# One transfer queue taking loads and stores in turns, and a looped TensorE program, in a per-sample matmul with residual

## The chip, the cores and the metric

The kernel runs on one core of a Trainium2 chip. The metric is the device time of one execution in microseconds. Three executions of the kernel before gave a median of 328.17 us (328.01 to 328.28). A further execution was recorded by the hardware profiler; it took 328.11 us. The profile's span, from the first to the last instruction that it shows, is 326.2 us, so 1.9 us of that execution lie outside the span.

## The reference

`x` is 128 samples of 128 channels by 1024 time steps, float32 (67.1 MB). Each sample has a subject number from 0 to 7, and each subject has a 128x128 float32 weight matrix. The sample is multiplied by the transposed matrix of its subject, and the product is added to the sample:

```python
w = weights[subjects]                       # (128, 128, 128): one matrix per sample
out = jnp.einsum('bct,bcd->bdt', x, w)      # per sample: w^T (d x c) times x (c x t)
return x + out
```

Every sample has to be read from HBM once and written back once: 134.2 MB together, to which the weights add 0.5 MB.

## The kernel before

A tile of the work is two samples (`G = 2`), 1 MB, and there are `NT = 64` tiles. One sample of a tile is 512 KB: 128 partitions of 1024 floats. Tiles live in 23 slots of SBUF (`SLOTS`, line 32); the result is written in place over the loaded samples, and the slot is then stored. PSUM holds four products of 128x1024 floats (`P_SLOTS`), and four buffers hold the weight matrix of a sample (`W_SLOTS`).

Each engine has its own instruction stream, written out by hand, and the streams meet only at semaphores:

- **SyncE (SP)** first loads all eight weight matrices (line 127), then issues two 512 KB loads per tile (lines 128 to 140). For the first 23 tiles it keeps a lead of three: before it issues tile i it waits until tile i-3 has landed (line 133). From tile 23 on it waits until the store that last used the slot has landed (line 131).
- **GpSimd (POOL)** reads the sample's subject number into a register (line 148), and copies that subject's matrix into one of the four weight buffers (line 158). From the fifth sample on it first waits until the product that used the buffer four samples ago is done (line 157).
- **TensorE (PE)** waits for the tile's load (line 145), the weight copy (line 160) and, from the fifth sample on, for the PSUM buffer to be free (line 162). It then does two matmuls of 128x512 (line 164). A float32 matmul shows as two MATMUL records in the profile, so one tile is eight of them. Its program is written out in full: 256 matmuls in a row. Three matmuls on zeros run ahead of it (line 111).
- **VectorE (DVE)** adds the product in PSUM to the sample in its slot, 128x1024 (line 174).
- **ScalarE (ACT)** issues one 1 MB store per tile when both its samples have been added (lines 177 to 183).

Thus loads sit in SP's DMA queue and stores in ACT's. Both queues are served by the same 16 DMA engines. In the profile, all loads and stores of samples carry line 53, which is the helper `transfer`; SP's are loads, ACT's are stores. At the end SP waits for the last 23 stores (line 187).

For one of the 16 DMA engines, a tile's load is four packets of 16 KB, and a tile's store is eight packets of 8 KB.

Of the kernel before, what the change touches and what calls it, by code (L numbers as in the profile page):

```python
# [1 line left out]

# [4 lines left out]

F32 = mybir.dt.float32
I32 = mybir.dt.int32
ALU = mybir.AluOpType


G = 2

N = 512  # L30

SLOTS = 23

W_SLOTS = 4
P_SLOTS = 4
DMA = 16

LEAD = 3

IDLE = 3  # L40

ROWS = 4
QUEUES = {mybir.EngineType.SP: "qSPDynamicHW", mybir.EngineType.Activation: "qActDynamicHW"}


def transfer(nc, engine, out, in_):

    later, nc._always_lower_symbolic_ap = nc._always_lower_symbolic_ap, False  # L50
    ins, outs = engine.lower_ap_dma(in_), engine.lower_ap_dma(out)
    nc._always_lower_symbolic_ap = later
    return engine.add_instruction(  # L53
        mybir.InstDMACopy(
            name=nc.get_next_instruction_name(),
            engine=engine.engine,
            ins=ins,
            outs=outs,
            mode="Copy",
            cce_op=ALU.bypass,  # L60
            queue=QUEUES[engine.engine],
        )
    )


@with_exitstack
def kernel(
    ctx: ExitStack,
    tc: tile.TileContext,
    x: bass.AP,  # L70
    subjects: bass.AP,
    weights: bass.AP,
    out: bass.AP,
):
    nc = tc.nc
    B, C, T = x.shape
    S, _, D = weights.shape
    NT = B // G

    def sbuf(name, *shape, dtype=F32):  # L80
        return ctx.enter_context(nc.sbuf_tensor(name, list(shape), dtype)).ap()

    given, near, wrap, index = (
        sbuf(name, 1, B, dtype=I32) for name in ("given", "near", "wrap", "index")
    )
    w_all = sbuf("w_all", C, S, D)
    ws = [sbuf(f"w{i}", C, 1, D) for i in range(W_SLOTS)]
    zeros = sbuf("zeros", C, N)
    xs = [sbuf(f"x{i}", C, G, T) for i in range(SLOTS)]
    ps = [  # L90
        ctx.enter_context(nc.psum_tensor(f"ps{i}", [D, T], F32)).ap() for i in range(P_SLOTS)
    ]

    s_given = tc.alloc_semaphore("s_given")
    s_wall = tc.alloc_semaphore("s_wall")
    s_index = tc.alloc_semaphore("s_index")
    s_zeros = tc.alloc_semaphore("s_zeros")
    s_copied = tc.alloc_semaphore("s_copied")
    s_product = tc.alloc_semaphore("s_product")
    s_added = tc.alloc_semaphore("s_added")  # L100
    s_load = [tc.alloc_semaphore(f"s_load{i}") for i in range(SLOTS)]
    s_store = [tc.alloc_semaphore(f"s_store{i}") for i in range(SLOTS)]

    with tc.tile_critical():  # L104

        nc.scalar.dma_start(given, subjects.rearrange("(o b) -> o b", o=1)).then_inc(s_given, DMA)

        nc.vector.memset(zeros, 0.0).then_inc(s_zeros, 1)  # L108
        nc.tensor.wait_ge(s_zeros, 1)
        for _ in range(IDLE):  # L110
            nc.tensor.matmul(  # L111
                ps[P_SLOTS - 1][:, :N], zeros[:, :D], zeros, start=True, stop=True
            )

        nc.vector.wait_ge(s_given, DMA)
        nc.vector.tensor_scalar(near, given, -S, S - 1, ALU.max, ALU.min).then_inc(s_index, 1)  # L118
        nc.vector.wait_ge(s_index, 1)
        nc.vector.tensor_scalar(wrap, near, 0, S, ALU.is_lt, ALU.mult).then_inc(s_index, 1)  # L120
        nc.vector.wait_ge(s_index, 2)
        nc.vector.tensor_tensor(index, near, wrap, ALU.add).then_inc(s_index, 1)  # L122
        nc.gpsimd.wait_ge(s_index, 3)

        nc.sync.dma_start(w_all, weights.rearrange("s c d -> c s d")).then_inc(s_wall, DMA)  # L127
        for i in range(NT):
            k, turn = i % SLOTS, i // SLOTS
            if turn:  # L130
                nc.sync.wait_ge(s_store[k], DMA * turn)
            elif i >= LEAD:
                nc.sync.wait_ge(s_load[k - LEAD], DMA * G)
            for g in range(G):
                transfer(
                    nc,
                    nc.sync,
                    xs[k][:, g, :],
                    x[i * G + g].rearrange("(a r) t -> a (r t)", r=ROWS),
                ).then_inc(s_load[k], DMA)  # L140

        nc.gpsimd.wait_ge(s_wall, DMA)
        for i in range(NT):
            k, turn = i % SLOTS, i // SLOTS
            nc.tensor.wait_ge(s_load[k], DMA * G * (turn + 1))
            for g in range(G):
                b = i * G + g
                s = nc.values_load(
                    index[0:1, b : b + 1],
                    engines=[mybir.EngineType.Pool],  # L150
                    min_val=0,
                    max_val=S - 1,
                    skip_runtime_bounds_check_because="the index is clamped on the chip above",
                )
                w, p = ws[b % W_SLOTS], ps[b % P_SLOTS]
                if b >= W_SLOTS:
                    nc.gpsimd.wait_ge(s_product, b - W_SLOTS + 1)
                nc.gpsimd.tensor_copy(w, w_all[:, bass.ds(s, 1), :]).then_inc(s_copied, 1)  # L158

                nc.tensor.wait_ge(s_copied, b + 1)  # L160
                if b >= P_SLOTS:
                    nc.tensor.wait_ge(s_added, b - P_SLOTS + 1)
                for t in range(0, T, N):
                    mm = nc.tensor.matmul(  # L164
                        p[:, t : t + N],
                        w[:, 0, :],
                        xs[k][:, g, t : t + N],
                        start=True,
                        stop=True,
                    )  # L170
                mm.then_inc(s_product, 1)

                nc.vector.wait_ge(s_product, b + 1)
                nc.vector.tensor_tensor(xs[k][:, g, :], p, xs[k][:, g, :], ALU.add).then_inc(  # L174
                    s_added, 1
                )
            nc.scalar.wait_ge(s_added, (i + 1) * G)
            transfer(
                nc,
                nc.scalar,  # L180
                out[i * G : (i + 1) * G].rearrange("g d t -> d g t"),
                xs[k].rearrange("d (o g) t -> d o (g t)", o=1),
            ).then_inc(s_store[k], DMA)


        for i in range(NT - SLOTS, NT):
            nc.sync.wait_ge(s_store[i % SLOTS], DMA * (i // SLOTS + 1))


# [1 line left out]
_INS = ["x", "itok_B_0_7", "L0_cond_weights"]  # L191
_OUTS = [((128, 128, 1024), "float32")]


# [20 lines left out]
```

## Time and profile before

| what | value |
|---|---|
| median of three executions | 328.17 us |
| the profiled execution | 328.11 us |
| its span | 326.2 us |
| moved by DMA | 134.86 MB, 413 GB/s over the span |
| TensorE, matmuls | 239.9 us busy, 74% |
| VectorE | 157.9 us busy, 48% |
| GpSimd | 37.8 us busy, 12% |
| DMA engines | busy in 38 of 40 slices of the span at nine tenths or more |

The page cuts the span into 40 slices of 8.15 us. The row "DMA" gives how busy the 16 DMA engines are in each, in tenths, and the row "GB/s" what they moved. The matmul row of TensorE counts pipelined instructions whose ends are modelled, so its busy share overstates how close that engine is to its limit. The queues in the page are numbered: q1 carries SP's transfers (loads and weights), q10 ACT's (stores), and q8 and q14 carry instructions that engines fetch while they run.

### The profile page before, as it was taken

How to read it: one execution, taken by the hardware profiler on the slowest of the kernel's cores; microseconds unless marked ns; L12 is line 12 of the kernel's file. 1: busy time of each engine (PE TensorE's matmuls, PEld its weight loads, DVE VectorE, ACT ScalarE, POOL GpSimd, SP SyncE). 2: the span in 40 equal slices, each digit the busy share in tenths (PEclk: the TensorE clock that was granted, in tenths of full speed). 3: DMA queues.
4: the chain of work that ended last, by engine and by line, in shares of the span. 5: the costliest groups of instructions: out<-in, count | busy, mean ns of one | idle time of the engine just before them, and what ended most of it. 6: DMA issues, size and time to landing. Idle time of an engine off the chain costs nothing.

```text
span 326.2 us, 1941 instructions
## 1 busy us (share of the span) xinstructions
PE 239.9 (74%) x518; PEld 94.5 (29%) x518; DVE 157.9 (48%) x132; POOL 37.8 (12%) x132
## 2 busy tenths in 40 slices
PE   6999989889899998998898898898776866000000
PEld 2444333333333333333333333333232322000000
DVE  1676665565565555665565565666445446000000
POOL 1111111111111111111111111111111110000000
PEclk9999999999999999999999999999999999655555
DMA  7999999999999999999999999999999999999993
GB/s 259 418 415 424 423 420 425 421 430 422 427 424 423 422 426 421 426 424 427 425 425 422 425 427 420 425 424 422 424 432 430 420 422 424 428 424 428 424 428 163
DMA packets 16411, 134.86 MB, mean 413 GB/s; under 512 B 3089, under 2 KB 4114, under 8 KB 4114
## 3 DMA queue, kind: packets, MB, share of 16 engines
q1 hardware_dynamic: 7184, 67.64, 49.5%
q10 hardware_dynamic: 9218, 67.11, 49.1%
q8 instruction: 4, 0.07, 0.1%
q14 instruction: 5, 0.04, 0.0%
HBM read 67.63 MB, written 67.11 MB: 413 GB/s over the span
## 4 chain that ended last, share of the span: by engine, by line
DMA 45%; SPq 24%; another core or an unknown queue 13%; PE 1%; issue 1%; DVE 0%
DMA x<-in_x_dram 30%; SPq L53 23%; DMA out_dram<-x 15%; PE ps L164 1%; DVE x L174 0%; SPq L127 0%; SPq L211 0%; SPq L104 0%
## 5 line engine op out<-in xcount | busy, mean ns | idle before, releaser
L164 PE MATMUL ps<-x,w 128*128 128x512 f32 x512 | 234.7, 604 | 34.2 <-DMA x<-in_x_dram 34.1
L174 DVE TENSOR_TENSOR x<-ps,x 128x1024 f32<-128x1024 f32 x128 | 156.7, 1224 | 117.4 <-PE ps L164 117.4
L164 PEld LDWEIGHTS ps<-x,w 128*128 128x128 f32 x512 | 92.6, 189 | 176.7 <-issue 95.2
L158 POOL COPY w<-w_all 128x128 f32 x128 | 37.6, 294 | 228.3 <-PE ps L164 222.3
L111 PE MATMUL ps<-zeros 128*128 128x512 f32 x6 | 5.2, 1035 | 1.7 <-DVE zeros L108 1.7
L111 PEld LDWEIGHTS ps<-zeros 128*128 128x128 f32 x6 | 1.8, 328 | 3.7 <-issue 2.1
L108 DVE MEMSET zeros<- 128x512 f32 x1 | 0.5, 485 | 1.1 <-SPq L104 1.1
L118 DVE TENSOR_SCALAR near<-given 1x128 int32<-1x128 int32 x1 | 0.2, 215 | 0.6 <-DMA given<-in_itok_B_dram 0.6
L122 DVE CUSTOM_DVE_ANT_0 index<-near,wrap 1x256 uint16<-1x256 uint16 x1 | 0.3, 278 | 0.0
L120 DVE TENSOR_SCALAR wrap<-near 1x128 int32<-1x128 int32 x1 | 0.2, 215 | 0.0
L202 POOL MEMSET const-float32-0.0<- 128x1 f32 x1 | 0.1, 98 | 0.2 <-issue 0.2
L202 POOL MEMSET const-bfloat16-1.0<- 128x1 bf16 x1 | 0.1, 102 | 0.0
L202 POOL MEMSET const-uint8-127<- 128x1 uint8 x1 | 0.1, 102 | 0.0
L202 POOL MEMSET const-float32-1.0<- 128x1 f32 x1 | 0.1, 98 | 0.0
## 6 DMA issues: line engine op xcount, KB each, us to landing
x<-in_x_dram SPq DMA_DIRECT2D x128, 512.0 KB, 12.0
out_dram<-x ACTq DMA_DIRECT2D x64, 1024.0 KB, 40.6
w_all<-in_L_cond_weights_dram SPq DMA_DIRECT2D x1, 512.0 KB, 4.3
given<-in_itok_B_dram ACTq DMA_DIRECT2D x1, 0.5 KB
```

Source lines behind the costliest of these rows:

```text
L53: return engine.add_instruction(mybir.InstDMACopy(name=nc.get_next_instruction_name(), engine=engine.engine, ins=ins, outs=outs, mode="Cop ...
L108: nc.vector.memset(zeros, 0.0).then_inc(s_zeros, 1)
L111: nc.tensor.matmul(ps[P_SLOTS - 1][:, :N], zeros[:, :D], zeros, start=True, stop=True)
L118: nc.vector.tensor_scalar(near, given, -S, S - 1, ALU.max, ALU.min).then_inc(s_index, 1)
L120: nc.vector.tensor_scalar(wrap, near, 0, S, ALU.is_lt, ALU.mult).then_inc(s_index, 1)
L122: nc.vector.tensor_tensor(index, near, wrap, ALU.add).then_inc(s_index, 1)
L158: nc.gpsimd.tensor_copy(w, w_all[:, bass.ds(s, 1), :]).then_inc(s_copied, 1)
L164: mm = nc.tensor.matmul(p[:, t : t + N], w[:, 0, :], xs[k][:, g, t : t + N], start=True, stop=True,)
L174: nc.vector.tensor_tensor(xs[k][:, g, :], p, xs[k][:, g, :], ALU.add).then_inc(s_added, 1)
L202: nc = _bacc.Bacc("TRN2", target_bir_lowering=False, num_devices=1)
```

## The change

All transfers of samples go into SP's queue. SP first issues the loads of five tiles (`LEAD = 5`). Then, for each tile i, it issues the load of tile i+5, and after it the store of tile i. There are 8 slots instead of 23, so from tile 8 on, the load of tile i+5 waits until the store of tile i-3 has landed. The waits of the first loads for earlier loads are gone. ScalarE issues only the one load of the subject numbers.

TensorE's program becomes a loop of 8 turns over a body of 8 slots, 16 samples or 32 matmuls. As the body has to be the same in each turn, its waits can't count upwards. A new helper, `take`, waits until a semaphore has reached a count and then lowers it by that count. TensorE no longer waits for the PSUM buffer itself. Instead GpSimd's copy of the weights of sample b waits until the addition of sample b-4 is done (it was: the product of sample b-4), and TensorE waits for that copy.

```diff
-SLOTS = 23
+SLOTS = 8
-LEAD = 3
+LEAD = 5
-QUEUES = {mybir.EngineType.SP: "qSPDynamicHW", mybir.EngineType.Activation: "qActDynamicHW"}
+QUEUES = {mybir.EngineType.SP: "qSPDynamicHW"}
+def take(engine, sem, count):
+    engine.sem_inc(sem, -count).wait_op(sem, count, "sem-ge")
...
-        for i in range(NT):
+        def load(i):
             k, turn = i % SLOTS, i // SLOTS
             if turn:
                 nc.sync.wait_ge(s_store[k], DMA * turn)
-            elif i >= LEAD:
-                nc.sync.wait_ge(s_load[k - LEAD], DMA * G)
             for g in range(G):
                 transfer(nc, nc.sync, xs[k][:, g, :], ...).then_inc(s_load[k], DMA)
+        def store(i):
+            k = i % SLOTS
+            nc.sync.wait_ge(s_added, (i + 1) * G)
+            transfer(nc, nc.sync, out[i * G : (i + 1) * G]..., xs[k]...).then_inc(s_store[k], DMA)
+        for i in range(LEAD):
+            load(i)
+        for i in range(NT):
+            if i + LEAD < NT:
+                load(i + LEAD)
+            store(i)
+        with nc.tensor.Fori(0, NT // SLOTS):
+            for k in range(SLOTS):
+                take(nc.tensor, s_load[k], DMA * G)
+                for g in range(G):
+                    j = k * G + g
+                    take(nc.tensor, s_copied, 1)
+                    for t in range(0, T, N):
+                        mm = nc.tensor.matmul(ps[j % P_SLOTS][:, t : t + N], ws[j % W_SLOTS][:, 0, :], xs[k][:, g, t : t + N], start=True, stop=True)
+                    mm.then_inc(s_product, 1)
...
-            nc.tensor.wait_ge(s_load[k], DMA * G * (turn + 1))
...
                 if b >= W_SLOTS:
-                    nc.gpsimd.wait_ge(s_product, b - W_SLOTS + 1)
+                    nc.gpsimd.wait_ge(s_added, b - W_SLOTS + 1)
...
-                nc.tensor.wait_ge(s_copied, b + 1)
-                if b >= P_SLOTS:
-                    nc.tensor.wait_ge(s_added, b - P_SLOTS + 1)
-                for t in range(0, T, N):
-                    mm = nc.tensor.matmul(...)
-                mm.then_inc(s_product, 1)
...
-            nc.scalar.wait_ge(s_added, (i + 1) * G)
-            transfer(nc, nc.scalar, out[...], xs[k]...).then_inc(s_store[k], DMA)
```

## The prediction

> **What bounds the kernel now.** I read the page's row of slices first, then the queues, then stretches of the start, the middle and the end, the waits and the order of time near the last load. The page:
>
> ```profile
> DMA  7999999999999999999999999999999999999993
> GB/s 259 418 415 424 423 420 425 421 430 422 427 424 423 422 426 421 426 424 427 425 425 422 425 427 420 425 424 422 424 432 430 420 422 424 428 424 428 424 428 163
> q1 hardware_dynamic: 7184, 67.64, 49.5%
> q10 hardware_dynamic: 9218, 67.11, 49.1%
> q8 instruction: 4, 0.07, 0.1%
> q14 instruction: 5, 0.04, 0.0%
> ```
>
> The DMA engines are full from the second slice to the last but one. 134.86 MB at 424 GB/s are 318.1 us of the 326.2. The rest is start and end. Stretches of the trace (stretch, its length, clock, DMA share, GB/s):
>
> ```profile
> 6.00:14.00 8.00, 1.00 0.99 406
> 40.00:140.00 100.00, 1.00 1.01 424
> 140.00:264.00 124.00, 1.00 1.01 424
> 285.00:318.00 33.00, 0.50 1.01 426
> 320.00:322.00 2.00, 0.50 0.52 217
> 322.00:324.00 2.00, 0.50 0.07 29
> 324.00:326.20 2.20, 0.50 0.00 0
> ```
>
> Three things are to be seen. Loads alone (6 to 14 us) run at 406, stores alone (285 to 318) at 426, both mixed from two queues at 424. The end is ragged: engines run dry from 320 us on, and from 322 to 324 us only 29 GB/s move, which is one engine's share (426/16 = 26.6). One straggler thus ends some 1.7 us after the other fifteen: in the trace's records of single packets its last packet ends at 324.1, the next engine's at 322.4, and nine engines end between 320.0 and 320.8. Then 2.1 us pass to the end of the span, and 1.9 us lie outside it (328.11).
>
> Near the last load, TensorE waits for data although it has the time (start, duration, and in brackets the idle time before):
>
> ```profile
> 267.12 3.70 PE L164 MATMUL ps<-x,w 128*128 128x512 f32 x8 [1.25 <-DMA x<-in_x_dram]
> 272.04 3.70 PE L164 MATMUL ps<-x,w 128*128 128x512 f32 x8 [1.22 <-DMA x<-in_x_dram]
> 275.78 1.23 DVE L174 TENSOR_TENSOR x<-ps,x 128x1024 f32<-128x1024 f32 x1 [0.49 <-PE ps L164]
> ```
>
> A tile takes TensorE 3.70 us of each 4.92. After it nothing computes; the last 48 us are stores. So only three things count: the rate of the 16 DMA engines, whether they ever lack work, and the ragged end.
>
> [...] the trace makes it depend on whether a load behind a store in the same queue runs like the mix or like loads alone. I go by the trace. [...] The q8 row shows four packets of 16 KB; their records lie at 44, 110, 177 and 226 us, near 1.05 us each. TensorE has the longest program (518 MATMUL and 518 LDWEIGHTS records[...]), so I take q8 to be its fetches; the page doesn't name the engine. [...]
>
> **The change part by part**, from 328.11.
>
> *Bytes.* The same. 0 us.
>
> *The queue's depth.* The order in the queue is load i+4, store i-1, then load i+5 once store i-3 has landed. Behind store i-3 stand load i+3, store i-2, load i+4 and store i-1: 4 MB, 9.9 us at 424. In that time the landing must be seen and the next load reach the engines. Issue to first packet took 1.7 us at the start (SP's first issue at 0.96, first packets at 2.7), the issue itself 0.6 us; for the landing of a store I allow 2 us, the length of the whole stretch between last packet and end of span. 4.3 us, and up to 3.3 us more for the spread between engines (320.8 to 324.1): 7.6 of 9.9. No gap: 0 us. SP's issues: 64 x (2 x 0.6 + 0.6) = 115 us of 316. Issues took up to 9.2 us before where a queue had no room; then the queue is full of work, and it costs nothing.
>
> *Stores wait on SP instead of ACT.* Behind the wait for the additions of tile i stand load i+6 and all that follows. Load i landed five loads and five stores' time before its store is due: 5 MB lie between, 12.4 us, and TensorE's 3.70, VectorE's 1.2 and the queueing before them need some 7. Nothing waits: 0 us. At the start: tiles 0 to 5 and the weights are 6.8 MB, at 406 GB/s until 2.7 + 16.7 = 19.4 us; the first store was issued at 12.86 before, and comes no later. At the end, behind the last load stand five stores, 12.4 us, against 7 us of compute: covered.
>
> *TensorE's loop.* Three lowered semaphores per tile and one branch per 8 tiles. No row shows either. Below 0.25 us each (PEld's waits for issue were at most 0.2 us), 0.8 us per tile beside 1.22 us idle; even without that cover the 12.4 - 7 us above take it. 0 us. [...]
>
> *Weights copied after the addition.* The copy of sample b now comes 1.2 us (VectorE) and 0.3 us (the copy) after product b-4; three products of 1.71 us lie between. 0 us.
>
> *Rate.* Unknown, bounded by packets. A 16 KB load packet took 640 ns while only loads ran, 616 in the mix; an 8 KB store packet 311 in either case. Now one engine gets four load packets, then eight store packets. Lower bound: the fastest mix seen early, 611 and 309, for all: 64 x (4 x 5 + 8 x 2) ns = 2.3 us less. Upper bound of rate alone: 640 for all; 24 of 256 load packets per engine were at 640 already, so 232 x 24 ns = 5.6 us more. Which? In the start, after a packet that was held up (839 to 1054 ns), the same engine did the next two to four load packets at 611 before it fell back to 640. [...] the lead lasts up to four load packets, just as many as a tile has. In the mix, one store packet between load packets was enough to keep them at 616. So I take eight stores to restore the lead: 616 and 311 as before, 0 us, with the two bounds kept.
>
> *Turning.* A queue turns 128 times between loads and stores. In the mix each engine turned some 500 times between the two queues with no gap. At the first store, though, half of the engines showed one packet longer by 0.22 to 0.26 us. If every turn to stores cost that: 64 x 0.23 = 14.7 us. I take 0.
>
> *The ragged end.* The four packets of q8, 4.2 us together, would, on one engine, put it just where it is: 4.2 us before 324.1 is 319.9, where the other early engines end. If they go, the next engine ends the run: 322.4, 1.7 us less. Bounds: 0 (q8 is another engine's or still fetched) and 3.3 (all end by 320.8).
>
> Sum: 328.11 - 1.7 = 326.4. The profiled execution is 0.06 under the median, so 326.5.
>
> **Rivals.**
> 1. *All as taken* (chance 0.50): 326.5; own range 324.5 to 327.4. For it: 424 and 426 in the trace, the lone straggler and q8's size.
> 2. *The straggler stays, rate as before* (0.15): 328.1. For it: q8 isn't named, and another engine may take the part. Against: 4.2 us fits its lateness.
> 3. *Loads fall back to the rate of loads alone* (0.20): +5.6 - 1.7, 332.0. For it: 640 ns in all loads without stores between. Against: the packets at 611 after a hold. It decides slower as soon as more than a third of the load packets fall back (1.7 / 5.6 = 0.3).
> 4. *Each turn to stores costs 0.23 us* (0.10): 341. For it: the first store's packet. Against: the mix. Over 0.03 us per turn it ends slower.
> 5. *The slots are too few* (0.05): if landing and reissue took 12 us and not 7.6, 2 us would be missing in every 4 tiles, 16 x 2.1 = 34 us, or some part of it: about 345. Against: the sum above.
>
> **How the numbers follow.** The time is case 1's. A tenth may lie beyond either side; cases 4 and 5 (0.15) are left out above, and a few hundredths below: 324.3 to 333.5, which takes in cases 1 to 3. What this kernel's measurement can tell from no change is about 0.2%, 0.66 us. Faster: case 1 and a little of 2, 0.51. Same: most of 2 and the edge of 1, 0.15. Slower: 3, 4, 5, with little else, 0.34.
>
> **What would show it.** Right: one data queue with 134.8 MB, slices at 424 or more from the second to the last but one, q8 gone or at one packet, no stretch of 2 us near 29 GB/s at the end, TensorE waiting for loads, no wait of SP for an addition with the DMA share under 0.95. Load packets at 616 confirm the rate; at 640, or slices near 415, it is case 3. Dips in each slice at full-speed packets are case 4; DMA share well under 1 with SP waiting for stores is case 5. I am wrong most easily where I took the lead of reads to be restored by stores, since no trace of one mixed queue exists here.

## The result and the profile after

The changed kernel takes 329.15 us (median of 7 executions, 329.07 to 329.69), the kernel before 328.28 us beside it (327.77 to 328.32). The ratio is 1.0034, with a 95% interval of 1.0024 to 1.0043: slower by 0.9 us, where 1.7 us less were forecast. The profiled execution took 329.49 us, its span is 327.7 us.

The page of the changed kernel, slices and queues:

```profile
DMA  7999999999999999999999999999999999999991
GB/s 250 416 418 430 410 433 418 418 434 421 415 432 420 421 428 425 422 431 422 422 433 422 424 430 422 424 431 421 426 432 420 424 434 418 427 433 418 425 425 79
q1 hardware_dynamic: 16400, 134.75, 98.3%
q14 instruction: 6, 0.05, 0.0%
q10 hardware_dynamic: 2, 0.00, 0.0%
```

All samples go through q1, q8 is gone, and the DMA engines are as full as before. Stretches of the changed kernel (stretch, length, clock, DMA share, GB/s):

```profile
6.00:14.00 8.00, 1.00 0.97 399
40.00:140.00 100.00, 0.98 1.01 424
140.00:264.00 124.00, 1.00 1.01 426
318.00:320.00 2.00, 0.50 1.00 422
320.00:322.00 2.00, 0.50 0.43 180
322.00:324.00 2.00, 0.50 0.06 25
324.00:326.00 2.00, 0.50 0.04 16
326.00:327.70 1.70, 0.50 0.02 5
```

The rate in the middle is 424 to 426 GB/s, against 424 for the mix of two queues. The difference is at the end: about one engine's share (25 GB/s; a sixteenth of 426 is 26.6) now moves not only from 322 to 324 us, but on to 325.4, where the last packet ends. The waits of SP's queue in the changed kernel (who waits, for whom, total, times, longest):

```profile
SPq L53 <- DMA out_dram<-x: 179.3, 56, 3.5
SPq L53 <- DVE x L200: 21.8, 9, 4.4
SPq L206 <- DMA out_dram<-x: 8.9, 4, 2.4
```

SP waits 56 times for a store to land, and nine times for an addition, while the DMA share stays at 1: these waits cost nothing that shows.

A store's semaphore is raised sixteen times, and the trace keeps the time of each (3088 times for the 193 transfers of SP in the changed kernel). They are read here as one for each of the 16 DMA engines. The last store's sixteen times say where the end comes from. "Middle" is the median of the sixteen, "last" the last of them, in us from the span's start:

| kernel | middle | last | last - middle | profiled execution |
|---|---|---|---|---|
| before | 321.19 | 324.48 | 3.29 | 328.11 |
| changed | 321.21 | 325.78 | 4.57 | 329.49 |

The middle engine ends at the same time. The straggler ends 1.3 us later, and the profiled execution is 1.4 us longer. Fifteen of the sixteen engines are done by 322.50. The lag of the last engine behind the middle one, from store to store in the changed kernel, is 0.34 us at tile 4, 1.03 at tile 16, 1.95 at tile 20, 2.84 at tile 32 and 4.47 at tile 56. From tile 20 on it grows by 0.07 us with every tile, and before that lies one step: 1.20 us at tile 18, 1.86 at tile 19, beside an instruction fetch of 8 KB on q14 at 117.4 us. The kernel before has a step of some 0.6 us too (tile 17, fetches of q14 at 125.9 and 126.5 us), and a growth of 0.07 to 0.08 us per tile between tiles 17 and 31, so neither is new. The growth stops when the last loads have landed (306 us in the middle engine): 4.60 at tile 60, 4.57 at tile 63.

### The profile page after: what moved, and what is told of

Same layout as the page of the kernel before. It is cut to its first block, busy times and chain, and to the rows that moved or that the text cites. A ratio compares the mean times of both kernels' runs of the same rounds, so it can differ in the third digit from the quotient of the medians.

```text
span 327.7 us, 2017 instructions
## 1 busy us (share of the span) xinstructions
PE 240.0 (73%) x518; PEld 95.1 (29%) x518; DVE 158.0 (48%) x132; POOL 38.1 (12%) x132
```

## The experiments

### Is it GpSimd's register loads, or TensorE's loop?

The subject numbers lie in one SBUF partition, and each of the 128 register loads reads there. The guess (theory R) was that this burdens one DMA engine alone; no run shows how partitions and DMA engines belong together. Four kernels: without the register loads (from the changed kernel and from the one before), with the register loads spread over 16 partitions, and with TensorE's program written out.

```diff
# e1_static, e2_before_static
-                s = nc.values_load(index[0:1, b : b + 1], ...)
+                s = b % S
...              (the copy then takes w_all[:, s : s + 1, :])
# e3_rotate: given ... index on 128 partitions, subjects broadcast to them
+                r = 64 * (b % 2) + 4 * (b // 2 % 8)
-                    index[0:1, b : b + 1],
+                    index[r : r + 1, b : b + 1],
# e4_unrolled
-        with nc.tensor.Fori(0, NT // SLOTS):
-            for k in range(SLOTS):
-                take(nc.tensor, s_load[k], DMA * G)
+            for i in range(NT):
+                k, turn = i % SLOTS, i // SLOTS
+                nc.tensor.wait_ge(s_load[k], DMA * G * (turn + 1))
                 for g in range(G):
-                    j = k * G + g
-                    take(nc.tensor, s_copied, 1)
+                    j = i * G + g
+                    nc.tensor.wait_ge(s_copied, j + 1)
...
```

> The changed kernel without GpSimd's register loads: the matrix of sample b is that of subject b modulo 8, known when the program is built, so the weights are not those of the sample's subject. Theory R (the 128 register loads from the subject numbers, which all lie in SBUF partition 0, slow the one DMA engine[...] by some 0.036 us each): the straggler goes, the last DMA engine ends some 1 us after the others and not 4.6, and the time falls by 3 to 4 us, to 325 to 326. Theory M (one DMA engine is slower in a mix of loads and stores whatever GpSimd does): no change, 329.0 to 329.4, 16 to 25 GB/s still moving between 322 and 326 us.

> The same edit in the kernel before (matrix of subject b modulo 8, so not that of the sample's subject). Theory R: its straggler (3.3 us after the middle engine) goes too, and it ends within 1.5 us of the others: 326 to 327. Theory M: 328.0 to 328.4 as before.

> The changed kernel with the subject numbers copied to all 128 partitions, and each register load taking another one of 16 partitions in turn[...]. Theory R: the delay of 4.6 us is shared by 16 engines, 0.3 us each: 325 to 326.5. Theory M: 329.0 to 329.4.

> The changed kernel with TensorE's program written out in full again, with rising wait counts (one queue, 8 slots, weights copied after the addition stay). If the loop of TensorE has a part in the loss: a time other than 329.15 by over 0.5 us, faster if it costs. If the loop only removed instruction fetches: the four 16 KB packets come back, each holding up one DMA engine by about 0.8 us, and the time is 329 to 331, by which engine they meet.

| kernel | median | ratio to before, 95% |
|---|---|---|
| e1_static | 329.10 | 1.0026 to 1.0054 |
| e2_before_static | 327.81 | 0.9988 to 1.0004 |
| e3_rotate | 329.72 | 1.0041 to 1.0068 |
| e4_unrolled | 329.19 | 1.0021 to 1.0048 |

The register loads are not the cause: theory R falls in all three. Without them the last engine still ends 4.40 us behind the middle one (e1_static) and 2.90 (e2_before_static). (In e3_rotate one engine is 2.2 us behind at tile 0 already; the broadcast of the subject numbers is probably why, and it is slower still.) TensorE's loop is worth nothing: written out, the time is 329.19 against 329.15. Its queues:

```profile
q1 hardware_dynamic: 16400, 134.75, 98.2%
q8 instruction: 4, 0.07, 0.1%
q14 instruction: 6, 0.05, 0.0%
q10 hardware_dynamic: 2, 0.00, 0.0%
```

q8 is back, so these four fetches are TensorE's, and they don't set the end: its last engine ends at 325.70 with them, and the changed kernel's at 325.78 without. Their records lie at 80, 145, 215 and 295 us, and the sixteen times of the stores show that each sets back another engine than the straggler, whose lag is, for example, 2.98 us at tile 24 and 2.96 at tile 25, before and after the second. That takes away the forecast's 1.7 us.

### One queue, or few slots?

```diff
# e5_two_queues_8, from the kernel before
-SLOTS = 23
+SLOTS = 8
# e6_one_queue_23, from e4_unrolled
-SLOTS = 8
+SLOTS = 23
+        ahead = LEAD
         for i in range(NT):
-            if i + LEAD < NT:
-                load(i + LEAD)
+            for _ in range(2 if ahead - i < SLOTS - 3 else 1):
+                if ahead < NT:
+                    load(ahead)
+                    ahead += 1
             store(i)
```

> The kernel before with 8 slots instead of 23, two queues as before. Theory S (one DMA engine loses some 0.07 us with each store that runs while loads are still running, in either kernel; with 23 slots 41 stores run beside loads and 23 after the last load, with 8 slots 58 and 6): the straggler ends about 1.2 us later than before, 329.0 to 329.6, as the changed kernel. Theory Q (what costs is that loads and stores share one queue): 327.8 to 328.3 as before.

> One queue with TensorE's program written out, but 23 slots; two loads ahead of each store until the loads are 20 tiles ahead, so that some 20 stores run after the last load. Theory S: the straggler loses about what it lost before, 327.8 to 328.4. Theory Q: 329.0 to 329.5 as with 8 slots.

| | two queues | one queue |
|---|---|---|
| 23 slots | 1 (the kernel before) | 1.0023 (1.0013 to 1.0033) |
| 8 slots | 1.0015 (1.0009 to 1.0022) | 1.0034 (1.0021 to 1.0048), e4_unrolled |

TensorE's program is written out in all four; the two with one queue also copy the weights after the addition. Both expectations failed in their numbers, since each theory gave the whole loss to one half of the change. Each half alone loses something, and together they lose about the sum. With 8 slots and two queues the middle engine ends at 321.24 as before, and the last 3.68 us later instead of 3.29. With 8 slots and one queue (e4_unrolled) it is 321.09, and the last 4.61 us later. So at 8 slots both halves add to the straggler's lag: 0.39 us for the slots, 0.93 for the queue, each read from one execution. One queue with 23 slots has another shape: the middle engine ends at 322.83, and the last only 2.17 us later, less than before. Here the loss is rate: two loads stand between stores at first, and from 40 to 140 us it moves 420 GB/s, not 424.

### Does the straggler need the computation?

The whole computation left out, in one queue with 8 slots (e7_copy_only) and in two queues with 23 (e11_copy_two_queues); TensorE's products left out (e9_no_matmul); VectorE's additions left out (e10_no_add).

```diff
# e7_copy_only (e11_copy_two_queues: the same on ScalarE's queue)
-            nc.sync.wait_ge(s_added, (i + 1) * G)
+            nc.sync.wait_ge(s_load[k], DMA * G * (i // SLOTS + 1))
...              (the streams of TensorE, GpSimd and VectorE are gone)
# e9_no_matmul: no products; the addition waits for load and weights
-                nc.vector.wait_ge(s_product, b + 1)
+                if g == 0:
+                    nc.vector.wait_ge(s_load[k], DMA * G * (i // SLOTS + 1))
+                nc.vector.wait_ge(s_copied, b + 1)
# e10_no_add: no additions; store and weights wait for the product
-            nc.sync.wait_ge(s_added, (i + 1) * G)
+            nc.sync.wait_ge(s_product, (i + 1) * G)
-                    nc.gpsimd.wait_ge(s_added, b - W_SLOTS + 1)
+                    nc.gpsimd.wait_ge(s_product, b - W_SLOTS + 1)
...
```

> One queue, 8 slots, with the whole computation left out: each tile is stored as it was loaded, once it has landed; TensorE, VectorE (but for the start) and GpSimd do nothing. If the straggler comes from DMA traffic alone it is still there, 4 to 5 us after the middle engine, growing by some 0.07 us per tile, and the time is 328.5 to 329.5. If it comes from what the engines do in SBUF, it goes, all DMA engines end within 1.5 us, and the time is 325 to 326.

> One queue, 8 slots, with TensorE's products left out: VectorE adds a PSUM buffer of zeros, GpSimd still copies the weights. Theory T (the part of the straggler's loss that copying alone doesn't show, some 0.04 of 0.07 us per tile, comes with TensorE's work, which has most of the instructions): the straggler loses 0.03 us per tile and the time is 326.5 to 327.5, as for copying alone. Theory V (it comes with VectorE's additions): 0.06 to 0.07 us per tile and 328.5 to 329.3.

> One queue, 8 slots, with VectorE's additions left out: TensorE makes every product and the loaded samples are stored unchanged. Theory T: the straggler still loses 0.06 to 0.07 us per tile, 328.5 to 329.3. Theory V: 0.03 us per tile, 326.5 to 327.5. A share of the loss in each of the two runs would mean that it goes by the number of instructions or of accesses, not by the engine.

> The kernel before, two queues and 23 slots, with the whole computation left out (each tile is stored as it was loaded). If one queue with 8 slots costs 0.9 us more than two with 23 whatever is computed: 326.0 to 326.5 against 327.0 for copying through one queue. If the cost needs the computation beside it: 326.8 to 327.2, the same as one queue.

| kernel | median | middle | last | profiled execution | profiled less last |
|---|---|---|---|---|---|
| e11_copy_two_queues | 326.10 | 321.24 | 322.48 | 326.06 | 3.58 |
| e7_copy_only | 327.00 | 321.56 | 324.30 | 327.97 | 3.67 |
| e9_no_matmul | 327.69 | 321.34 | 324.31 | 328.03 | 3.72 |
| e10_no_add | 328.95 | 321.15 | 325.30 | 329.02 | 3.72 |
| changed | 329.15 | 321.21 | 325.78 | 329.49 | 3.71 |

In each of them 3.6 to 3.7 us pass between the straggler's last store and the end of the execution, and the middle engine hardly moves. So the straggler sets the time. (The profiled execution of e7_copy_only is the longest of its six, 1 us over the median; its lag is therefore more than the usual one.) The end of the two copying kernels, one queue first:

```profile
320.00:322.00 2.00, 0.50 0.53 221
322.00:324.00 2.00, 0.50 0.06 25
324.00:326.20 2.20, 0.50 0.02 4
```

```profile
320.00:322.00 2.00, 0.50 0.43 180
322.00:324.00 2.00, 0.50 0.00 0
324.00:327.70 3.70, 0.69 0.01 2
```

In one queue the share of a single engine still moves from 322 to 324 us, in two queues nothing does. Copying through one queue costs 0.9 us more than through two: e11_copy_two_queues's first expectation, though 23 and 8 slots differ here too. The straggler is still there when only copying, so it needs no computation, but it grows by less than half as much: both expectations of e7_copy_only fail. The growth through one queue, per tile from tile 32 to tile 56: 0.030 us when only copying (2.01 to 2.74), 0.043 without products (1.97 to 2.99), 0.060 without additions (2.66 to 4.11), 0.068 with all (2.84 to 4.47). Neither TensorE nor VectorE brings it alone, so the last sentence of e10_no_add's expectation applies, and the next question is whether instructions or data do it.

### Instructions, or data?

```diff
# e14_copy_tiny, from e7_copy_only (and a buffer "tiny" in SBUF)
+        for i in range(NT):
+            nc.vector.wait_ge(s_load[i % SLOTS], DMA * G * (i // SLOTS + 1))
+            for j in range(26):
+                nc.vector.memset(tiny[:, 26 * i + j : 26 * i + j + 1], 0.0)
...
# e15_copy_wide, from e7_copy_only: two per tile, each waiting for the one before
+                nc.vector.memset(wide, 0.0).then_inc(s_added, 1)
```

> Copying through one queue with 8 slots (the whole computation left out), with 26 tiny writes of VectorE (128x1) per tile, 1664 in all, which touch almost no data. Theory I (what the computation adds to the straggler's loss goes by the number of instructions that run, whatever they move): from 0.03 to 0.06 or 0.07 us per tile, last DMA engine 4 us or more behind the middle one, 328.3 to 329.3. Theory A (it goes by the data that the engines move in SBUF): 0.03 us per tile and 326.5 to 327.5, as without them.

> The same copying with two writes of VectorE per tile of 128x2048, 128 in all, each about as long as two additions and with as much data. Theory I: 0.03 us per tile, 326.5 to 327.5. Theory A: 0.05 us or more per tile, 327.7 to 329.

e15_copy_wide: 327.24 us, as copying alone (327.00), though VectorE is busy for seven tenths of the time; the engine that ends last falls behind by 0.030 us per tile (1.33 us at tile 32, 2.04 at tile 56). So the data that VectorE writes add nothing to the lag, and theory A falls. e14_copy_tiny: 351.07 us, ratio 1.0677 to 1.0719, which neither theory has. Rows of its page, and stretches of it (the last column of each stretch is GB/s):

```profile
PE 5.0 (1%) x6; PEld 1.8 (1%) x6; DVE 26.0 (7%) x1668; POOL 0.2 (0%) x4
GB/s 255 415 414 421 434 425 419 426 429 426 419 426 425 426 424 419 424 431 420 368 393 353 387 394 343 397 360 357 364 381 381 372 386 364 363 372 381 421 394 22
q14 instruction: 15, 0.12, 0.1%
```

```profile
40.00:140.00 100.00, 7.73 (x518) 0.50 1.01 424
140.00:180.00 40.00, 2.93 (x191) 0.50 1.01 407
180.00:264.00 84.00, 5.72 (x390) 0.50 0.99 372
```

e7_copy_only, which has no such writes, has this row instead:

```profile
q14 instruction: 2, 0.02, 0.0%
```

Tiny instructions that are busy for 7% of the span, and move next to nothing, cost 24 us. But q14, the queue of fetched instructions, has 13 packets of 8 KB more (15 against 2), one for each 128 of the 1664 writes: what they do move is their own code. Set beside the stores' times, up to the point where the rate falls, they are where the time is lost:

| fetch on q14, us | lag of the last engine before it | and after it |
|---|---|---|
| 30.4 | 0.83 (tile 1) | 1.88 (tile 2) |
| 55.9 | 1.80 (tile 6) | 2.80 (tile 7) |
| 81.4 | 2.78 (tile 11) | 3.74 (tile 12) |
| 107.0 | 3.75 (tile 16) | 5.01 (tile 17) |
| 132.7 | 4.89 (tile 21) | 5.67 (tile 22) |
| 158.7 | 6.00 (tile 26) | 7.00 (tile 27) |

The lag jumps by 0.8 to 1.3 us at each fetch, though the record of a fetch is only 309 to 313 ns long. Between fetches it doesn't grow (1.88 us at tile 2, 1.80 at tile 6; 2.80 at tile 7, 2.78 at tile 11), although 26 writes run with each tile; the one other rise is from 5.54 to 6.00 us at tile 26. So in this kernel the lag rises with the fetches of instructions, and not with their running.

Until 165 us the kernel still moves 422 to 428 GB/s. Then, at a lag of 7 us, the rate falls. The next load waits for a store to land on all sixteen engines, so it may be that the other fifteen run out of issued work. No run shows this. The trace doesn't show them idle: the DMA share stays at 0.99, and load packets take 764 ns in the mean between 180 and 264 us, against 616 in e7_copy_only. The last engine itself slows from 5.13 us per tile (tiles 2 to 27) to 5.63 (tiles 32 to 56), which further fetches of 1 us per five tiles don't explain. That part is open.

This experiment is no answer for the straggler of the changed kernel. That one grows slowly from tile 20 on, with no fetch at each rise. It is probably another DMA engine, too. A fetch at 117 to 121 us in the kernels with one queue and 8 slots (120.7 in e14_copy_tiny) is probably SP's, for the page of e7_copy_only counts only 20 instructions on TensorE, VectorE and GpSimd together. It sets the changed kernel's straggler back, but not the last engine of e14_copy_tiny (4.97 us at tile 19, 4.75 at tile 20). The slow growth does rise with the number of instructions on record: 0.030 us per tile with 269 (e7_copy_only) and with 460 (e15_copy_wide), 0.043 with 869 (e9_no_matmul), 0.060 with 1889 (e10_no_add), 0.068 with 2017 (changed); kernels in which fetches move the middle engine too are left out. That is theory I as a correlation and no more. Whether the instructions, their semaphores or the profiler's records of them load that engine was not told apart; every execution of these runs has a span from the profiler, so no time here is free of its records.

### Do turns cost?

```diff
# e12_turn_each, from e4_unrolled: SLOTS = 16, LEAD = 10, nothing else
# e13_turn_two, from e12_turn_each
-        for i in range(NT):
-            if i + LEAD < NT:
-                load(i + LEAD)
-            store(i)
+        for i in range(0, NT, 2):
+            for h in (i, i + 1):
+                if h + LEAD < NT:
+                    load(h + LEAD)
+            for h in (i, i + 1):
+                store(h)
```

> One queue, TensorE's program written out, 16 slots and a lead of 10 tiles; loads and stores take turns with each tile as in the changed kernel. A reference for the next run. The straggler loses some 0.07 us per tile as with 8 slots, but over 53 tiles (the last 10 stores have no load beside them): 3.9 us behind the middle engine; ten tiles of loads alone at the start cost 0.4 us more than five: 328.8 to 329.3.

> The same with turns half as often: two tiles' loads, then two tiles' stores. If the straggler's loss belongs to the turn from loads to stores in one queue: half of it per tile, 0.035 to 0.04 us, and 1.5 us less than the run with a turn per tile. If it belongs to each store or load that runs while the other kind is under way: 0.07 us per tile and the same time within 0.3 us.

e12_turn_each took 329.17 us (1.0022 to 1.0051), as expected; its last engine ends 3.55 us after the middle one. e13_turn_two took 330.00 us (1.0043 to 1.0077): half as many turns are slower by 0.8 us, and both expectations fail. The straggler's lag is smaller, 2.49 us, but the middle engine ends at 323.49 instead of 321.62. Stretches from 20 to 40, 40 to 140 and 140 to 264 us, one tile per turn first:

```profile
20.00:40.00 20.00, 1.00 1.01 414
40.00:140.00 100.00, 1.00 1.01 424
140.00:264.00 124.00, 1.00 1.01 426
```

```profile
20.00:40.00 20.00, 1.00 1.00 410
40.00:140.00 100.00, 0.97 1.01 420
140.00:264.00 124.00, 0.90 1.01 424
```

With two tiles per turn an engine gets eight load packets of 16 KB in a row. Between 40 and 80 us they take 641 ns in the mean, and 623 from 100 to 200 us; with four in a row it is 618 and 617. Loads alone took 640 ns in the median before (6 to 14 us). So part of the rate of loads alone comes back with blocks twice as long, as the prediction's idea of a lead (up to four load packets at 611 ns before a fall to 640) would have it. That stores give such a lead was an estimate, and no run shows it directly.

## Why the prediction was right or wrong

**Bytes, queue depth, stores on SP.** Right. The DMA share is 1.00 or 1.01 in every stretch between 20 and 320 us, with SP waiting 179 us for stores and 22 us for additions. The 9.9 us of work behind a store (4 MB at 424 GB/s) were enough for landing, reissue and lag: the changed kernel's lag stays below 5 us, and e14_copy_tiny keeps its rate up to a lag of 7 us. (The 5 MB between load i and the wait for store i are two loads and three stores, not five of each.)

**TensorE's loop and the later weight copies.** Right at 0 us: loop against written-out program is 329.15 against 329.19. That TensorE fetches no more once it loops was an estimate, and it held: the changed kernel has no row of q8, e4_unrolled has four packets there. The later copies were not undone alone; the engines' waits for them lie beside a full DMA share (1.00 or 1.01).

**Rate.** Right. The median load packet took 616 ns and the median store packet 311 in both kernels, and the middle engine ends at 321.21 against 321.19. At first, from 20 to 80 us, load packets took 622 to 624 ns in the mean, later 617. The reason given, that eight stores restore a lead for four loads, was an estimate. It fits e13_turn_two, where what rival 3 feared appears in part at blocks twice as long (641 ns in the mean between 40 and 80 us). (The trace before has 17 load packets of 256 per engine at 634 ns or more, not 24 at 640; that moves the upper bound by less than 0.2 us.) This was the point named as the likeliest to fail, and it held.

**Turning.** Right at 0 us: half as many turns gained nothing (330.00 us against 329.17).

**The ragged end.** Wrong, and the failing step: "The four packets of q8, 4.2 us together, would, on one engine, put it just where it is". They were TensorE's fetches and they did go, but they did not lie on the straggler: with them e4_unrolled ends no later (325.70) than the changed kernel without (325.78). The coincidence of 4.2 us with its lateness was taken for a cause. Each of the before's stores has sixteen times in the trace, and these could have told. After the fetches at 44, 110 and 177 us another engine than the straggler is set back (at the first, the last engine is 0.46 us behind the middle at tile 3 and 1.26 at tile 4, then stays there), and the straggler gets late by itself, 0.07 to 0.08 us with each tile. (After tile 31 the lags before swing up to 6.3 us at tile 40 and back to 3.2 at tile 43, where the last loads land; with loads and stores in two queues they can't be read there as lost time, and the fourth fetch, at 226 us, can't be placed.)

What the forecast had as -1.7 us measured +1.3 us in the profiled executions: the straggler's lag went from 3.29 to 4.57 us. At 8 slots both halves of the change feed it (0.39 and 0.93 us). Few slots let loads run to 306 us instead of 271, and the lag grew only while loads ran (4.60 us at tile 60, 4.57 at tile 63); why one queue makes it grow more, and what makes it grow at all, stays open.

**The rivals.** Rival 2 (the straggler stays, 328.1) came nearest, without its growth. Adding the measured 1.3 in place of -1.7 to the sum gives 329.4 against the profiled 329.49. No rival had the straggler growing: the prediction looked at the end in the last stretches alone, and did not follow it back through the run.

## What to carry to other kernels

The DMA engines of the changed kernel were full from 20 to 320 us (a share of 1.00 or 1.01), and its execution ended 3.71 us after the last store of the slowest of the sixteen. In such a kernel, follow each engine's landings through the whole run, and not the mean rate, before you name what makes one of them late. A stretch at the end that moves a sixteenth of the full rate (here 25 of 426 GB/s) is the sign of it. A cause whose size fits is still a guess until the same lag is seen to rise at its events: here the four fetches had the right size and lay on other engines. The same look at every store, beside the times of the fetches, told steps from slow growth in e14_copy_tiny, where the mean of 0.2 us per tile looks like a price of running instructions until the steps are seen.

## What the runs showed of the hardware

- In e14_copy_tiny one DMA engine's lag rose by 0.8 to 1.3 us at each of six 8 KB instruction fetches, whose records are 309 to 313 ns long. 1664 writes of 128x1 on VectorE, 26 us of busy time, made 351.07 us of e7_copy_only's 327.00, whose DMA share is 1.01. 128 writes of 128x2048 cost nothing measurable (e15_copy_wide, 327.24).
- One DMA engine of the sixteen fell behind by 0.03 us per tile of 2 MB moved when only copying (e7_copy_only), and by 0.07 us with all the computation beside it (the changed kernel). The cause is open.
- Loads alone ran at 391 (e6_one_queue_23) to 406 GB/s (the kernel before) between 6 and 14 us, stores alone at 426 (the kernel before, 285 to 318 us). In the changed kernel four 16 KB load packets followed each eight store packets and took 616 ns in the median, 617 in the mean after the first 80 us. With eight in a row (e13_turn_two) the mean was 641 ns between 40 and 80 us and 623 from 100 to 200 us.
- In the changed kernel a lag of one engine of up to 4.6 us went with a rate of 423 to 428 GB/s between 40 and 318 us. In e14_copy_tiny, with 4 MB (9.9 us) queued behind the store that a load waits for, the rate fell from 424 to 372 GB/s after the lag had reached 7 us. Why is open.
